# A two-layer attention network on one core: bias table in array quarters, short statistics as GpSimd powers, a reordered feed-forward

## The chip, the cores and the metric

The kernel runs on one core of a Trainium2 chip. The metric is the device time of one execution in microseconds (us). A core has five engines that run their own instruction queues in order: TensorE (PE, matrix products), VectorE (DVE), ScalarE (ACT, functions by table), GpSimd (POOL) and SyncE (SP, which here issues most DMAs). Matrix products go to PSUM; everything else works in SBUF.

## The reference, cut to what matters

The input is eight images of 384 channels by 32 x 32 pixels, so N = 1024 tokens each, in float32.

```python
# layer 0: group norm (32 groups), attention with 8 heads of 48 and a relative bias
qkv = tokens(_gn(x)) @ qkv_w + qkv_b
attn = softmax(q * 48**-0.5 @ k.T + bias)      # bias[h, q, k] = gelu(rel @ mlp_w1 + b1) @ mlp_w2 + b2
x = x + from_tokens((attn @ v) @ proj_w + proj_b)
# layer 1: layer norm, attention with 6 heads of 64, q and k normalised per head (mean 0, std 1)
t = tokens(x)
t = t + attention(_ln_t(t))
# feed-forward on the layer norm of t: two products with sign weights, each followed by a scaling
h = gelu(clip(y1 * 128 / (max|y1| + 1e-5)))     # y1 = u @ sign(W1 - mean).T + b1, 384 -> 1536
t = t + clip(y2 * 128 / (max|y2| + 1e-5))       # y2 = h @ sign(W2 - mean).T + b2, 1536 -> 384
```

The scalings take the largest value over groups of images of size 8 // 5 = 1, five groups; images 5 to 7 get zeros from the feed-forward, which the kernel leaves out for them. `bias` depends only on the difference of two pixel positions, so it is a table of 63 x 63 = 3969 values a head, of which each (query, key) block reads a window.

## The kernel before, in words

All tiles have 128 partitions; a product tile of PSUM holds 128 x 1024 float32 and there are four of them in each layer. Both layers run under `manual_schedule`, so every engine runs its instructions in the order in which the program's text issues them. A helper `later` holds pieces of work: `later.after(n, f)` runs `f` at the n-th following `later.step()`, and a step is made after every product unit, projection or feed-forward step.

Tiles come from pools with a fixed number of buffers. In layer 0 the pool `a_e` has nine buffers (`etile`): the exponentials `e`, the windows `wide`, the broadcast reciprocals `rb` and the residuals `res` share them. In layer 1 the pool `b_work` has 17 (`wtile`). A tile takes a buffer at its first write in program order and gives it back after its last use in program order; the next tile to take that buffer waits for that last use.

**Layer 0, start.** `bias_table` (line 205) goes over the 3969 positions in eight pieces of 512. Each piece makes two products of the 2-row `rel` with `w1` (line 213), two gelus (L223), two products with `w2` into 8 rows (L230), an addition (L234) and a DMA to the table in DRAM. The steps of the first group norm are called between the pieces. Then `grow_part(h, c)` reads windows of the table: four DMAs into `wide` (L246) and one reversed copy into `grow`, on ScalarE for even `c` (L252) and VectorE for odd `c` (L254). There are 32 such parts; eight are read during the first projections and the others between the first image's score units, just before they are needed.

**Layer 0, each image.** There are 32 units: four pairs of heads by eight key tiles. `scores` makes the products of a unit (L361), VectorE adds the bias into an `e` tile (L369) and ScalarE takes the exponential (L373); `weigh` multiplies with `v` two units later (L384, `LAG = 2`). After a pair's last unit `weigh` copies the sums out (L393), sends the denominators through DRAM (`sd`, `sums`, L399 and L401), takes the reciprocal two steps later (L404), sends it through DRAM again (`rd`, L406) into a broadcast tile `rb` (L409), and two steps after that GpSimd multiplies (L410). The group norm of the next image (`group_norm`) takes its square root on ScalarE (L284). Then come the next image's projections (L316 for queries and keys, L339 for values) and, in the fourth unit of the next image, the output projection (L421).

**Layer 1.** `center` prepares the weights. Each image has 24 units (three pairs by eight), with scores L1028, exponentials L1035, running totals on VectorE (L1042, L1045) and weighing L1056; `divide` sums the totals by a product (L1068) and divides as in layer 0 (L1086 to L1095). `project_qk` (L894) also squares its result (L908) for `head_sums` (L917); `normalise_qk` turns these into scales through DRAM: sqrt L938, reciprocal L939, `rq` and `kc` loads, and multiplies on GpSimd (L968). `token_sums` (L864) and `token_stats` (L881 to L887) make the layer norm's statistics; `scale_v` multiplies the values by them (L990).

For the first five images the feed-forward follows the attention, with the next image's projections set between its parts: `project_out` (L1104), `layer_norm` (L1148, L1149, and `halves`, which splits a tile in a high part, L1122, and a low part, L1124, for two fast products), `feed_forward_1` (L1185, evicted by L1170, largest value L1173, all-reduce on GpSimd L1159), then `quantised_gelu` for each of twelve chunks (VectorE scales L1198, GpSimd clips on both sides L1199, ScalarE gelu L1200, `halves`) and `feed_forward_2` (L1212).

Of the kernel before, what the change touches and what calls it, by code (L numbers as in the profile page):

```python
# [93 lines left out]
def _layer0(tc, ins, x1, flag):  # L94
# [6 lines left out]
    with ExitStack() as ctx:  # L101
# [18 lines left out]
        gn_eps = const.tile([GROUPS, 1], F32, tag="gn_eps", name="gn_eps")  # L120
        nc.vector.memset(gn_eps, 1e-5)


# [3 lines left out]
        rel = v[0:2].rearrange("p m h d -> p (m h d)")[:, 0:NREL]  # L127
        nc.sync.dma_start(rel, ins["rel"])
# [7 lines left out]
        w1 = const.tile([2, HID], F32, tag="w1", name="w1")  # L136
        b1 = const.tile([HC, 2], F32, tag="b1", name="b1")
        w2 = const.tile([HC, 2, H0], F32, tag="w2", name="w2")
        b2 = const.tile([H0, 1], F32, tag="b2", name="b2")
        nc.scalar.dma_start(w1, ins["L0_conv_mlp_w1"])  # L140
        with nc.allow_non_contiguous_dma(reason="a bias, once"):
            nc.scalar.dma_start(b1, ins["L0_conv_mlp_b1"].rearrange("(k p) -> p k", p=HC))
        nc.scalar.dma_start(w2, ins["L0_conv_mlp_w2"].rearrange("(k p) h -> p k h", p=HC))
        nc.scalar.dma_start(b2, ins["L0_conv_mlp_b2"].unsqueeze(1))
# [60 lines left out]
        def bias_table(between):  # L205

            starts = list(range(0, NREL, HALF))

            def hidden(at):
                n = min(HALF, NREL - at)  # L210
                ph = mm2(f"ph{at}")
                for k in range(2):
                    nc.tensor.matmul(
                        ph[0:HC, k, :n], w1[:, ts(k, HC)], rel[:, at : at + n], start=True, stop=True
                    )
                return ph

            ph = hidden(starts[0])
            for i, at in enumerate(starts):
                n = min(HALF, NREL - at)  # L220
                hid = etile(f"hid{at}", (HC, 2, HALF))
                for k in range(2):
                    nc.scalar.activation(  # L223
                        hid[:, k, :n], ph[0:HC, k, :n], AF.Gelu, bias=b1[:, k : k + 1]
                    )
                if i + 1 < len(starts):
                    ph = hidden(starts[i + 1])
                pb = mm2(f"pb{at}")
                for k in range(2):
                    nc.tensor.matmul(  # L230
                        pb[0:H0, 0, :n], w2[:, k, :], hid[:, k, :n], start=(k == 0), stop=(k == 1)
                    )
                part = etile(f"part{at}", (H0, HALF))
                nc.vector.tensor_scalar_add(backwards(part[:, n - 1 : n], n), pb[0:H0, 0, :n], b2)  # L234
                nc.sync.dma_start(table[:, NREL - at - n : NREL - at], part[:, :n])
                if i < len(between):
                    between[i]()
# [18 lines left out]
        def group_norm(b, xn):  # L256
# [25 lines left out]
            def scatter():  # L282
                nc.vector.bn_aggr(mv, gs)
                nc.scalar.activation(mv[:, 1:2], mv[:, 1:2], AF.Sqrt, bias=gn_eps)  # L284
                nc.vector.reciprocal(mv[:, 1:2], mv[:, 1:2])
                nc.vector.tensor_scalar(
                    mv[:, 0:1], mv[:, 0:1], mv[:, 1:2], -1.0, ALU.mult, ALU.mult
                )
                nc.vector.tensor_copy(of, mv.unsqueeze(1).to_broadcast([GROUPS, C // GROUPS, 2]))
                with nc.allow_non_contiguous_dma(reason="statistics"):  # L290
                    nc.sync.dma_start(
                        back.rearrange("(g r) s -> g (r s)", g=GROUPS),
                        of.rearrange("g r s -> g (r s)"),
                    )
                    nc.sync.dma_start(sc, back.rearrange("(k p) s -> p k s", p=P))
# [81 lines left out]
        def weigh(b, u, es):  # L377
# [24 lines left out]

            def invert():
                nc.vector.reciprocal(inv, mine)  # L404
                with nc.allow_non_contiguous_dma(reason="sums"):
                    nc.sync.dma_start(rd.rearrange("j (p c) -> (j p) c", c=2 * N // P), inv)  # L406
                rb = etile(f"rb{b}_{pair}")
                for j in range(2):
                    nc.sync.dma_start(rb[ts(j, S0)], rd[j].partition_broadcast(S0))  # L409
                later.after(2, lambda: nc.gpsimd.tensor_mul(o, o, rb))  # L410

            later.after(2, invert)
# [18 lines left out]
        with tc.manual_schedule():  # L431
            stages = group_norm(0, first)
            load_weights_qk()
            between = [stages[0], stages[1], stages[2], load_weights_v_out, stages[3], None, stages[4]]
            bias_table([w or (lambda: None) for w in between])
            nc.gpsimd.memset(v, 1.0)
            parts = [(h, c) for h in range(H0) for c in range(4)]
            for i in range(4):
                later.after(i + 1, lambda: (grow_part(*parts.pop(0)), grow_part(*parts.pop(0))))
            qk = project_qk(0, first)  # L440
            project_v(0, first)
            for b in range(B):
                held = []
                for i, u in enumerate(units):
                    if b == 0 and parts and i > 1:
                        for _ in range(2 if i < 6 else 1):
                            grow_part(*parts.pop(0))
# [319 lines left out]
def _layer1(tc, ins, x1, out):  # L767
    nc = tc.nc
    with ExitStack() as ctx:
# [46 lines left out]
        eps = const.tile([P, 1], F32, tag="eps", name="eps")  # L816
        nc.vector.memset(eps, 1e-5)
# [61 lines left out]
        def token_stats(name, c):  # L879

            nc.vector.tensor_scalar_mul(c, c, 1.0 / C)  # L881
            mean, var = c[:, 0], c[:, 1]
            sq = small.tile([P, MT], F32, tag="tq", name="tq" + name)
            nc.vector.tensor_mul(sq, mean, mean)
            nc.vector.tensor_sub(var, var, sq)
            nc.scalar.activation(var, var, AF.Sqrt, bias=eps)
            nc.vector.reciprocal(var, var)  # L887
# [37 lines left out]
        def normalise_qk(b, qk, d):  # L925
# [10 lines left out]

            def invert():
                nc.scalar.activation(c, c, AF.Sqrt, scale=1.0 / (D1 - 1))  # L938
                nc.vector.reciprocal(c, c)  # L939
                rqs = []  # L940
# [25 lines left out]
                def apply():  # L966
                    for pair in range(NP1):
                        nc.gpsimd.tensor_mul(qk[pair, 0], qk[pair, 0], rqs[pair])  # L968
                    nc.vector.tensor_scalar_mul(kc, kc, D1**-0.5)

                later.after(2, apply)

            later.after(2, invert)
            return kc

# [87 lines left out]
        def divide(b, oT, pair):  # L1063
# [20 lines left out]

            def invert():
                nc.vector.reciprocal(inv, inv)  # L1086
                with nc.allow_non_contiguous_dma(reason="sums"):
                    nc.sync.dma_start(spread(rd), inv)
                rb = wtile(f"rb{b}_{pair}")
                for j in range(2):  # L1090
                    nc.sync.dma_start(rb[ts(j, D1)], rd[j].partition_broadcast(D1))
                if pair < NP1 - 1:
                    later.after(2, lambda: nc.gpsimd.tensor_mul(oT[:, pair], oT[:, pair], rb))
                else:
                    later.after(1, lambda: nc.vector.tensor_mul(oT[:, pair], oT[:, pair], rb))  # L1095

            later.after(2, invert)
# [22 lines left out]
        def halves(name, t, high):  # L1120
# [3 lines left out]
            nc.vector.tensor_sub(low, t, high.bitcast(F32))  # L1124
            return high, low

        def layer_norm(b, xt, c):
# [3 lines left out]
            rows, parts = [], []  # L1131

            def spread():
                token_stats(f"f{b}", c)
                nc.vector.tensor_mul(c[:, 0], c[:, 0], c[:, 1])
                r = dram.tile([2, N], F32, tag="lr", name=f"lr{b}")
                with nc.allow_non_contiguous_dma(reason="statistics"):
                    nc.sync.dma_start(bass.AP(r.tensor, r.offset, [[MT, P], [N, 2], [1, MT]]), c)
                shift, scale = wtile(f"ls{b}"), wtile(f"lc{b}")
                nc.sync.dma_start(scale, r[1].partition_broadcast(P))  # L1140
                nc.sync.dma_start(shift, r[0].partition_broadcast(P))
                rows.extend((scale, shift))

            def apply():
                for k in range(KC):
                    eng = nc.gpsimd if k == 0 else nc.vector
                    t = wtile(f"un{b}_{k}")
                    eng.tensor_mul(t, xt[:, k], rows[0])  # L1148
                    eng.tensor_sub(t, t, rows[1])  # L1149
                    parts.append(halves(f"un{b}_{k}", t, high[:, k]))  # L1150

            return parts, spread, apply
# [44 lines left out]
        def quantised_gelu(name, y, r):  # L1197
            nc.vector.tensor_scalar(y, y, r, 1.0, ALU.mult, ALU.mult)  # L1198
            nc.gpsimd.tensor_scalar(y, y, QTOP, -QTOP, ALU.min, ALU.max)  # L1199
            nc.scalar.activation(y, y, AF.Gelu)  # L1200
            return halves(name, y, work.tile([P, N], F32R, tag="w", name="h" + name))

        def feed_forward_2(b, y1, r, made, xt):
# [194 lines left out]
```

## Time and profile before

| | |
|---|---|
| runs of before, us | 3776.57, 3784.86, 3781.83; median 3781.83 |
| profiled execution, us | 3782.44 |
| its span from the first to the last instruction, us | 3780.5 |
| mean granted TensorE clock | 0.953 |
| PE busy | 3464.5 us, 92% |
| DVE busy | 1652.6 us, 44% |
| ACT busy | 1471.3 us, 39% |
| POOL busy | 360.0 us, 10% |

The stages in the trace: the bias table's products run from 3.8 to 58.3 us, the first projections of layer 0 start at 58.7, its first scores at 115.6, and the second image's projections at 290.0. The later images of layer 0 follow each other every 201 us. Layer 1's weights load at 1742.5. Its feed-forward images take about 291 us each.

How to read the lines that follow. A line of the timeline gives start and duration in us, engine, source line, instruction, what it writes and reads, shapes and the number of instructions; in brackets, how long the engine had been idle before it and what ended that. A line of the waits gives the engine and tile that waited, what it waited for, the total in us, the number of times and the longest. A line of the windows gives start:end, length, then the busy time of PE, weight loads, DVE, ACT and POOL with their instruction counts, the granted clock, the DMA share and GB/s. Busy digits are tenths.

### The profile page before, as it was taken

How to read it: one execution, taken by the hardware profiler on the slowest of the kernel's cores; microseconds unless marked ns; L12 is line 12 of the kernel's file. 1: busy time of each engine (PE TensorE's matmuls, PEld its weight loads, DVE VectorE, ACT ScalarE, POOL GpSimd, SP SyncE). 2: the span in 40 equal slices, each digit the busy share in tenths (PEclk: the TensorE clock that was granted, in tenths of full speed). 3: DMA queues.
4: the chain of work that ended last, by engine and by line, in shares of the span. 5: the costliest groups of instructions: out<-in, count | busy, mean ns of one | idle time of the engine just before them, and what ended most of it. 6: DMA issues, size and time to landing. Idle time of an engine off the chain costs nothing. (4 is left out here: it accounts for less than half of the span.)

```text
span 3780.5 us, 31094 instructions
## 1 busy us (share of the span) xinstructions
PE 3464.5 (92%) x12170; PEld 1452.6 (38%) x12170; DVE 1652.6 (44%) x1667; ACT 1471.3 (39%) x1460; POOL 360.0 (10%) x259
## 2 busy tenths in 40 slices
PE   9889999999999999996987898799698698699998
PEld 2224343433333343432434434435334434434342
DVE  1452635353544445362434443543453453363434
ACT  2341524243433425250433443442453452352533
POOL 1010000000000001000100200200200200201010
PEclk9889999999999999998998999899899899899999
DMA  3321011010101010102300100100110010011011
GB/s 86 85 70 40 29 34 40 18 56 8 62 12 63 12 57 18 40 18 83 91 12 12 52 18 12 52 18 12 33 32 18 24 40 18 18 46 42 29 41 35
DMA packets 100428, 140.34 MB, mean 37 GB/s; under 512 B 61912, under 2 KB 65378, under 8 KB 100270
## 3 DMA queue, kind: packets, MB, share of 16 engines
q1 hardware_dynamic: 97484, 138.24, 12.6%
q8 instruction: 98, 1.61, 0.2%
q14 instruction: 58, 0.48, 0.0%
q10 hardware_dynamic: 2788, 0.02, 0.0%
HBM read 110.90 MB, written 27.32 MB: 37 GB/s over the span
## 5 line engine op out<-in xcount | busy, mean ns | idle before, releaser
L373 ACT ACTIVATE e<-e 128x1024 f32<-128x1024 f32 x512 | 538.5, 1056 | 655.1 <-DVE e L369 636.8
L369 DVE TENSOR_TENSOR e<-s,grow 128x1024 f32<-128x1024 f32 x512 | 600.4, 1216 | 269.0 <-PE s L361 226.9
L361 PE MATMUL s<-qk 48*128 48x512 f32 x2048 | 537.6, 623 | 34.0 <-DVE e L369 34.0
L1035 ACT ACTIVATE e<-s,kc 128x1024 f32<-128x1024 f32 x384 | 405.3, 1112 | 297.1 <-PE s L1028 276.6
L384 PE MATMUL o<-e,v 128*64 128x512 f32 x2048 | 502.8, 614 | 0.0
L1028 PE MATMUL s<-qk,qk 64*128 64x512 f32 x1536 | 398.8, 626 | 30.3 <-ACT e L1035 20.0
L1045 DVE TENSOR_TENSOR t<-t,e 128x1024 f32<-128x1024 f32 x288 | 352.3, 1268 | 167.2 <-ACT e L1035 167.2
L1056 PE MATMUL o<-e,v 128*64 128x512 f32 x1536 | 372.1, 608 | 0.0
L361 PEld LDWEIGHTS s<-qk 48*128 48x128 f32 x2048 | 187.2, 188 | 378.2 <-DVE e L369 201.9
L316 PE MATMUL pq<-xn,wqk 128*128 128x512 f32 x768 | 331.7, 593 | 0.0
L894 PE MATMUL pq<-bx,L_attn_qkv_wT 128*128 128x512 f32 x576 | 257.2, 600 | 8.0 <-DVE L_attn_qkv_wT L851 8.0
L384 PEld LDWEIGHTS o<-e,v 128*64 128x64 f32 x2048 | 126.8, 137 | 345.4 <-issue 204.9
L1028 PEld LDWEIGHTS s<-qk,qk 64*128 64x128 f32 x1536 | 142.1, 189 | 279.9 <-ACT e L1035 159.3
L410 POOL TENSOR_TENSOR oT<-oT,rb 128x1024 f32<-128x1024 f32 x32 | 75.8, 2368 | 1543.2 <-DMA rb<-rd 1463.9
L316 PEld LDWEIGHTS pq<-xn,wqk 128*128 128x128 f32 x768 | 145.3, 190 | 186.2 <-issue 186.2
L1212 PE MATMUL y2p<-hyh,w 128*128 128x512 f32 x360 | 138.7, 472 | 69.5 <-ACT hyh L1122 69.4
L1056 PEld LDWEIGHTS o<-e,v 128*64 128x64 f32 x1536 | 94.7, 137 | 256.9 <-issue 254.6
L1124 DVE TENSOR_TENSOR lyh<-y,hyh 128x1024 fp32r<-128x1024 f32 x60 | 73.7, 1228 | 266.4 <-ACT hyh L1122 266.4
L421 PE MATMUL pp<-oT,wp 128*128 128x512 f32 x384 | 169.0, 600 | 13.4 <-POOLq L1351 13.4
L894 PEld LDWEIGHTS pq<-bx,L_attn_qkv_wT 128*128 128x128 f32 x576 | 108.8, 192 | 149.9 <-issue 138.9
L1185 PE MATMUL y1p<-un,w 128*128 128x512 f32 x360 | 122.4, 423 | 37.1 <-ACT un L1122 37.1
L1200 ACT ACTIVATE y<-y 128x1024 f32<-128x1024 f32 x60 | 63.4, 1057 | 224.4 <-POOL y L1199 224.4
(142 smaller groups left out, 2910.4 us busy)
## 6 DMA issues: line engine op xcount, KB each, us to landing
rb<-rd SPq DMA_DIRECT2D x112, 256.0 KB
wide<-table SPq DMA_DIRECT2D x128, 114.2 KB
xn<-in_x_dram SPq DMA_DIRECT2D x24, 512.0 KB
res<-in_x_dram SPq DMA_DIRECT2D x24, 512.0 KB
x<-res SPq DMA_DIRECT2D x24, 512.0 KB
bx<-x SPq DMA_DIRECT2D x8, 1536.0 KB
rq<-hi SPq DMA_DIRECT2D x48, 256.0 KB
out_dram<-bx SPq DMA_DIRECT2D x24, 512.0 KB
```

The source lines that it names most:

```text
L316: nc.tensor.matmul(pq[:, h], wqk[:, k, s * H0 + 2 * pair : s * H0 + 2 * pair + 2, :].rearrange("p h d -> p (h d)"), xn[:, k, ts(h, HALF)], ...
L361: nc.tensor.matmul(s[j][:, h], qk[pair][rows, 1, ts(mt, P)], qk[pair][rows, 0, ts(h, HALF)], start=True, stop=True,)
L369: nc.vector.tensor_add(e, flat2(s[j]), grow[:, 2 * pair + j, w0 : w0 + IH, :].rearrange("p w c -> p (w c)"),)
L373: nc.scalar.activation(e, e, AF.Exp)
L384: nc.tensor.matmul(po[ts(j, S0), h], v[:, mt, 2 * pair + j, :], es[j][:, ts(h, HALF)], start=(mt == 0), stop=(mt == MT - 1),)
L421: nc.tensor.matmul(pp[:, h], wp[:, k, ts(m, P)], oT[:, k, ts(h, HALF)], start=(k == 0), stop=(k == NP0 - 1),)
L894: nc.tensor.matmul(pq[:, h], wqkv[:, k, s * C + pair * P : s * C + (pair + 1) * P], xt[:, k, ts(h, HALF)], start=(k == 0), stop=(k == KC - 1),
L1028: nc.tensor.matmul(s[j][:, h], qk[pair, 1][rows, ts(mt, P)], qk[pair, 0][rows, ts(h, HALF)], start=True, stop=True,)
L1035: nc.scalar.activation(e, flat2(s[j]), AF.Exp, scale=kc[:, pair, j, mt : mt + 1])
L1045: nc.vector.tensor_add(total[pair, j], total[pair, j], e)
L1056: nc.tensor.matmul(po[ts(j, D1), h], v[:, mt, at : at + D1], es[j][:, ts(h, HALF)], start=(mt == 0), stop=(mt == MT - 1),)
L1212: nc.tensor.matmul(py[m][:, h], w2[:, k, ts(m, P)], parts[i][:, ts(h, HALF)], start=(k == 0 and i == 0), stop=(k == FC - 1 and i == 1),)
```

## The change

1. **Bias table.** `rel` and `w1` are loaded four times, at partitions 0, 32, 64 and 96, each copy of `rel` holding a quarter of the positions. The hidden products of four quarters use four row groups of the array; the output products write to four groups of 32 columns. The table is made in two rounds (`hidden`, `table_part`) with gelus of 96 x 1024. All 32 `grow_part`s are issued during the first projections, three a step for eight steps and two a step for four. `v`, whose memory held `rel`, is filled with ones at the start.
2. **Short statistics.** Square roots (ScalarE) with reciprocals (VectorE) become powers of -0.5, and the reciprocals of the divisions powers of -1, as two-input instructions on GpSimd: 128x16 in `weigh` and `divide`, 128x8 in `token_stats`, 128x96 in `normalise_qk`, 32x1 in `group_norm`. In `weigh` and in layer 1's first two divisions the power, the DMAs behind it, the allocation of `rb` and the multiply are issued at once instead of by `later`.
3. **Feed-forward image.** `layer_norm` issues its statistics at once and makes its chunks in `begin` and `end`, between the next image's projections. `Supply` takes `quantised_gelu` apart: in step k of `feed_forward_2` come the low half of chunk k+1, the gelu and high half of k+2 and the clips of k+3. VectorE clips above with the scaling; the lower clip is on VectorE for the first three chunks, else on GpSimd. The last two chunks' products are grouped by output tile. The last pair of query and key projections moves behind `feed_forward_1`, the value projections ahead of `project_out`, and the last head sums behind the first products of `feed_forward_2`; the power of `normalise_qk` is issued in its third step and the multiplies in steps seven to nine.
4. **Images without feed-forward** issue the normalisation at once, and their value projections behind it. The start of layer 1 does the same.

The diff's core:

```diff
-        w1 = const.tile([2, HID], F32, tag="w1", name="w1")
+        QT, QN = 32, 2 * HALF
+        rel = etile("rel")
+        w1 = const.tile([P, HID], F32, tag="w1", name="w1")
...
+        for g in range(P // QT):
+            at = g * QN
+            n = min(QN, NREL - at)
+            nc.sync.dma_start(rel[g * QT : g * QT + 2, 0:n], ins["rel"][:, at : at + n])
+            nc.scalar.dma_start(w1[g * QT : g * QT + 2], ins["L0_conv_mlp_w1"])
...
+                        nc.tensor.matmul(
+                            ph[0:HC, i], w1[g * QT : g * QT + 2, ts(k, HC)],
+                            rel[g * QT : g * QT + 2, ts(r, HALF)], start=True, stop=True,
+                        )
...
+                    nc.tensor.matmul(
+                        pb[ts(g, QT), 0], w2[:, k, :], hids[k, g // 2][:, g % 2],
+                        start=(k == 0), stop=(k == 1),
+                    )
...
+            stages[0]()
+            hids.append(hidden(1))
+            for r in range(2):
+                table_part(r, hids[r])
+                stages[1 + r]()
+            load_weights_v_out()
+            for stage in stages[3:]:
+                stage()
...
+            for i in range(12):
+                later.after(i + 1, lambda i=i: grow_parts(3 if i < 8 else 2))
...
-                    if b == 0 and parts and i > 1:
-                        for _ in range(2 if i < 6 else 1):
-                            grow_part(*parts.pop(0))
...
-            def invert():
-                nc.vector.reciprocal(inv, mine)
...
-                later.after(2, lambda: nc.gpsimd.tensor_mul(o, o, rb))
-
-            later.after(2, invert)
+                nc.gpsimd.tensor_tensor(inv, mine, over.to_broadcast([P, 2 * N // P]), ALU.pow)
+                nc.sync.dma_start(rd.rearrange("j (p c) -> (j p) c", c=2 * N // P), inv)
+            rb = etile(f"rb{b}_{pair}")
+            for j in range(2):
+                nc.sync.dma_start(rb[ts(j, S0)], rd[j].partition_broadcast(S0))
+            nc.gpsimd.tensor_mul(o, o, rb)
...
-                nc.scalar.activation(c, c, AF.Sqrt, scale=1.0 / (D1 - 1))
-                nc.vector.reciprocal(c, c)
+                nc.gpsimd.tensor_scalar(c, c, 1.0 / (D1 - 1), 0.0, ALU.mult, ALU.add)
+                nc.gpsimd.tensor_tensor(c, c, rsqrt.to_broadcast(list(c.shape)), ALU.pow)
...
+            def clip(self, k):
...
+                nc.vector.tensor_scalar(y, y, self.r, QTOP, ALU.mult, ALU.min)
+                if k < 3:
+                    nc.vector.tensor_scalar_max(y, y, -QTOP)
+                else:
+                    nc.gpsimd.tensor_scalar(y, y, -QTOP, 0.0, ALU.max, ALU.add)
...
             for k in range(FC):
...
+                supply.low(k + 1)
+                supply.gelu(k + 2)
+                supply.clip(k + 3)
+                if k < FC - 2:
+                    for m in range(KC):
+                        products(k, m)
+                if k == 0:
+                    between()
                 later.step()
...
+                    supply = Supply(b, *feed_forward_1(b, un))
+                    supply.clip(0)
+                    supply.clip(1)
+                    supply.gelu(0)
+                    project_qk(b + 1, 2, 0, ahead, nqk, sq)
+                    supply.low(0)
+                    supply.clip(2)
+                    supply.gelu(1)
+                    project_qk(b + 1, 2, 1, ahead, nqk, sq)
+                    ways = []
+
+                    def between():
+                        head_sums(b + 1, 2, sq, d)
+                        ways.extend(normalise_qk(b + 1, nqk, d))
+                        later.after(3, ways[1])
+                        for pair in range(NP1):
+                            later.after(7 + pair, lambda pair=pair: ways[2](pair))
+
+                    feed_forward_2(b, supply, between, xt)
```

## The prediction

> **What bounds the kernel now.** I read the page first, then what TensorE waits for, then windows by stage, then the timeline around each wait. Slices of busy time and of granted clock:
>
> ```profile
> PE   9889999999999999996987898799698698699998
> PEclk9889999999999999998998999899899899899999
> ```
>
> TensorE is 92% busy, so only its holes and the half-clock time behind them can be won: the third slice, and layer 1 in slices 18 to 35. Its waits (what waited, on what: total, times, longest):
>
> ```profile
> PE y2p L1212 <- ACT hyh L1122: 69.4, 29, 6.1
> PE hs L917 <- ACT qsq L908: 66.2, 7, 13.7
> PE y1p L1185 <- ACT un L1122: 37.1, 15, 2.7
> PE s L361 <- DVE e L369: 34.0, 11, 13.5
> ```
>
> Three of the four lie in the feed-forward, five times each; the fourth is layer 0's first image. What a hole costs beyond itself, from the timeline (start, length):
>
> ```profile
> 169.82 3.78 PE L361 MATMUL s<-qk 48*128 48x512 f32 x6 [4.03 <-DVE e L369]
> 173.53 3.68 PE L384 MATMUL o<-e,v 128*64 128x512 f32 x8
> ...
> 179.19 1.94 PE L384 MATMUL o<-e,v 128*64 128x512 f32 x8
> ```
>
> After 4.03 us idle, six score products take 3.78 us instead of 1.49 and eight others 3.68 instead of 1.94: 4.0 us more. I add 4.0 us to a hole of 4 us or more, 2.5 to one of 3 to 4, about half its length to one over 10. [...]
>
> Two stages by windows (length, TensorE busy, ..., clock, DMA share, GB/s): a feed-forward image, and an image of layer 0.
>
> ```profile
> 2354.40:2646.40 292.00, 252.31 (x926) 126.73 (x924) 129.09 (x131) 120.78 (x120) 37.56 (x29) 0.92 0.09 27
> 489.00:690.00 201.00, 200.65 (x706) 74.93 (x704) 93.44 (x93) 77.92 (x75) 13.01 (x7) 1.00 0.12 35
> ```
>
> The first loses 40 us idle and 7% of clock (20 us); the periods average 291 us, and I count 58 us to be won in each. The second loses nothing: layer 0 after its first image can only get worse.
>
> **1. Bias table and early reads: -70 us.** Table matmuls (64 instructions, 28.6 + 27.0 us busy) fill TensorE from 3.8 to 59 us. Their number stays, but four row or column groups work at once. The scores, which use two, do eight in 1.92 us (0.24 each) against 0.43 for the whole-array projection: 1.8 times; for four I take 4 at best, 2 at worst, 14 to 28 us. With eight gelus of 1.06 us between, and loads and memsets to 6 us, the table stands at 23. Group norm's last statistics and gather are issued behind it; gather 3.5, then from its aggregate to the applied image 5.1 us as now (43.8 to 48.9): projection at 33 (28 to 40), not 58.7. Then the 128 window reads of 114.2 KB, which ran before at this rate (a window of 70 us from 50, 40 slices):
>
> ```profile
> DMA  0000005499999998000000000000000000000079
> GB/s 0 9 0 0 9 7 193 127 253 234 224 234 234 228 233 194 0 0 0 0 0 0 0 0 0 0 0 0 0 0 0 0 0 0 0 0 0 0 204 412
> ```
>
> 14.6 MB at 230 GB/s is 64 us, from 31 to 95. Copies stand ahead of evictions on VectorE and ScalarE, so adds begin at 98; TensorE is by then two units ahead, and with 4 us of clock the loop starts in effect at 99.5, not 115.6: 16. The first image's loop lasted 174.4 us, against 120.1 in the second (140.7 less 20.6 of output projection): 54. If reads run as slowly as 40 did from 117 (29.7 us), 39 us is left of the 70; if only TensorE binds, 80.
>
> **2. Layer 0's divisions: +226 us.** The reciprocal becomes a power on GpSimd, and the chain loses its delays. But rb is now taken from the nine-buffer pool at the division and released there in program order. Slots come back first in, first out (so they do in the buffers of the kernel before): with six e tiles held, rb's slot goes to the first e three units later. Before, taken one unit later and released two after that, it came back at six. The second division in image 1:
>
> ```profile
> 437.99 1.99 PE L361 MATMUL s<-qk 48*128 48x512 f32 x8
> ...
> 439.64 0.99 ACT L393 COPY oT<-o 128x1024 f32<-128x1024 f32 x1
> ...
> 443.92 0.25 DVE L404 RECIPROCAL inv<-sums 128x16 f32<-128x16 f32 x1 [1.49 <-DMA sums<-sd]
> ...
> 447.64 2.36 DVE L369 TENSOR_TENSOR e<-s,grow 128x1024 f32<-128x1024 f32 x2 [1.27 <-PE s L361]
> ...
> 450.88 2.38 POOL L410 TENSOR_TENSOR oT<-oT,rb 128x1024 f32<-128x1024 f32 x1 [21.17 <-DMA rb<-rd]
> ```
>
> Weighing ends at 438.0; the multiply ends at 453.3, or 14.8 + p after it in clean chains, p the power of 128x16. The add of three units on stood at 447.6, so it waits on the multiply; queued behind it on VectorE are all further adds. TensorE needs that add's PSUM at 449.6 (11.6) and gets it at 14.8 + p + 1.2: 4.4 + p lost, plus 4.0 of clock. Three pairs in each of eight images, 24 chains; the fourth pair's falls under the next projection.
>
> No row shows a power. Nearest: GpSimd's two-input multiply, 2368 ns for 1024 (2.3 ns an element a partition); its library routine PARTITION_ALL_REDUCE takes 380 ns for one. A power is a logarithm and an exponential, some 25 such operations: I take 60 ns, so 0.5 us for 128x8, 1.0 for 128x16, 5.8 for 128x96 (ends 0.2 and 36). The chains then cost 24 x (4.4 + 1.0 + 4.0). [...]
>
> **3. Feed-forward: -245 us.** Now each of twelve steps is one serial loop of clip 0.75, GpSimd clip 1.04, gelu 1.06, cast 1.04, low half 1.23, as the next clip is queued behind the low half:
>
> ```profile
> 2347.15 0.38 POOL L1159 PARTITION_ALL_REDUCE qt<-qm  x1 [47.44 <-DVE qm L1157]
> 2354.89 1.03 POOL L1199 TENSOR_SCALAR y<-y 128x1024 f32<-128x1024 f32 x1 [7.36 <-PE hs L917]
> ...
> 2374.51 1.04 POOL L1199 TENSOR_SCALAR y<-y 128x1024 f32<-128x1024 f32 x1 [5.48 <-DVE y L1198]
> 2379.79 1.04 POOL L1199 TENSOR_SCALAR y<-y 128x1024 f32<-128x1024 f32 x1 [4.24 <-issue]
> ```
>
> That is 5.28 us a step; TensorE needs 2.80 (12 x 0.233). Spread over two steps it becomes 2.64: TensorE binds. GpSimd's 7.4 us after its all-reduce hides, as the first three clips run on VectorE (0.75 us each more) and the fourth is due 11 us later; two projections cover the rest, and the head sums (13.4 us wait) move behind the first products. The normalised chunks (7.9 us of waits) start a projection earlier: covered by about 1 us with the 0.5 power in the chain. The last pair's multiply, 1.95 us late now, has 12.0 us of cover for a chain of 11.95 (the tail's, sum to product) + 0.75: 1.3 lost. The 128x96 power stands among GpSimd's clips: 2.3 us are slack, 3.5 + 2.5 of clock lost; three multiplies of 2.4 beside clips of 1.04 in 2.8 us steps, 2. So 9 of the 58 stay: 49 x 5.
>
> **4. The rest: -10 us.** Images without feed-forward wait 7 us and 3.4 of clock for keys; after, cover 22.4 (sums, four value projections) against a chain of 19.8 + 6.3: 5.7 lost, -9 for two. Layer 1's start: 9.2 + 5 becomes 3 to 4 late plus clock, -7. In its first image the division blocks GpSimd between all-reduces of the sign weights; VectorE and ScalarE wait behind: 14 us instead of 8.3, +8. Layer 0's sqrt table loads lie on an idle ScalarE: nothing, but 0.35 a image, -2. Removing vector work gains nothing elsewhere (44% busy).
>
> Sum: -70 + 226 - 245 - 10 = -99. The profiled execution took 3782.4 (span 3780.5), 0.6 over the median: **3684 us**.
>
> **Rivals.** *The power decides (slower).* At 170 ns an element, 128x96 takes 16 us: feed-forward keeps 27 of 58 (-155), chains 12.1 each (+290), images without feed-forward +22, layer 1's start +7, first image +10, with -72 left of term 1 and the rest: +102, 3884. Between the two cases the sum moves 1.8 us a ns, so it decides from about 115 ns (11 us for 128x96). [...]
> *No slot wait.* If rb's slot returns later than I count, term 2 is gone: 3458. For it: layer 0 shows no wait of this kind now; against: the order of slots follows from the program.
> *Cheap power.* At 20 ns: chains 214, feed-forward 54 x 5, -95 for the rest: 3631; part of the forecast's range.
> *Early reads do not help* (slow reads, copies blocking evictions): 31 us more, 3715.
>
> **Chances.** Forecast with its bounds 0.48, power above its point 0.36, about even 0.06, no slot wait 0.10. The range 3600 to 3890 leaves out the no-wait case and the longest powers, under 0.2; the forecast alone spans 3610 to 3750. Changes of 0.2% (7.6 us) are what a measurement can tell. Faster 0.58, same 0.05, slower 0.37.
>
> **What would show it.** First scores near 98 us and no copies after them; 24 waits of s on e of 4 to 6 us in layer 0, with adds released by GpSimd's multiply three units after a division; powers near 1.0 and 5.8 us; y2p, hs and y1p waits under 30 us together. Wrong if layer 0 stays without waits, or if GpSimd's powers exceed 10 us.

## The result, and the profile after

The changed kernel takes 3888.12 us (median of four runs, 3884.31 to 3894.01) where the kernel before, on the same chip, takes 3783.11: a ratio of 1.0282, 95% interval 1.0264 to 1.0301. It is slower by 105 us; the forecast was 3684, 99 us faster. The profiled execution took 3884.31 (span 3882.5).

The page of the changed kernel, slices of TensorE's busy time and granted clock:

```profile
PE   7999999999999999996788798698798798698988
PEclk9999998999999998997889899899899899899999
```

The hole in the third slice is gone; layer 1 (from slice 20) has as many holes as it had. What TensorE waits for in the changed kernel (total, times, longest; `y2p` is the second feed-forward product, `s` a unit of scores, `hs` the head sums):

```profile
PE y2p L1253 <- ACT hy L1136: 127.6, 30, 16.2
PE s L379 <- DVE e L387: 65.3, 25, 3.7
PE s L1050 <- POOL qk L992: 52.9, 3, 18.7
PE hs L941 <- ACT qsq L932: 42.9, 17, 7.6
```

The waits on `un` (37.1 before) have left the top, and those on `qsq` shrank, but the second product waits 127.6 us instead of 69.4, layer 0's scores 65.3 over 25 places instead of 34.0, and the scores on their normalised queries up to 18.7 us. GpSimd's groups by shape tell why (busy us, mean ns of one):

```profile
L1230 POOL TENSOR_SCALAR y<-y 128x1024 f32<-128x1024 f32 x45 | 171.5, 3816 | 65.9 <-DVE y L1226 62.7 <-DMA rq<-hi 2.8
L965 POOL TENSOR_TENSOR hc<-hc,rsqrt 128x96 f32<-128x96 f32 x8 | 125.3, 15667 | 0.7
L420 POOL TENSOR_TENSOR inv<-sums,over 128x16 f32<-128x16 f32 x32 | 93.0, 2905 | 1326.0 <-DMA sums<-sd 1326.0
L911 POOL TENSOR_TENSOR tcf<-tcf,rsqrt 128x8 f32<-128x8 f32 x5 | 8.3, 1664 | 0.4
L303 POOL TENSOR_TENSOR gmv<-gmv,rsqrt 32x1 f32<-32x1 f32 x8 | 4.5, 562 | 0.7
```

The powers of lines 303, 911, 420 and 965 take 562, 1664, 2905 and 15667 ns for 1, 8, 16 and 96 elements a partition: about 0.4 us and 155 to 160 ns an element, where the forecast took 60. (In two other places the shapes of 16 and 8 average 3158 and 2163 ns.) The clip of line 1230 is the other surprise: 3.82 us, where the kernel before had a clip of 1.04. GpSimd is busy 846.7 us instead of 360.0.

The same two stages as before, by windows (length, PE, weight loads, DVE, ACT, POOL, clock, DMA share, GB/s):

```profile
2354.40:2641.20 286.80, 246.52 (x925) 123.92 (x924) 136.78 (x120) 116.02 (x114) 97.91 (x43) 0.92 0.09 27
236.00:454.60 218.60, 211.13 (x707) 76.90 (x705) 92.81 (x87) 75.84 (x73) 25.71 (x15) 0.96 0.10 32
```

The feed-forward image is 5 us shorter than the window shown before (four periods average 287.8 against 291.3), and an image of layer 0, which lost nothing before, now takes 218.6 instead of 201. (A period is the time from one image's second product to the next one's.)

One division of layer 0, from the timeline of the changed kernel (start, length; weighing ends at 389.5):

```profile
391.12 0.99 ACT L411 COPY oT<-o 128x1024 f32<-128x1024 f32 x1
...
391.55 2.35 DVE L387 TENSOR_TENSOR e<-s,grow 128x1024 f32<-128x1024 f32 x2 [1.43 <-PE s L379]
...
395.34 2.36 DVE L387 TENSOR_TENSOR e<-s,grow 128x1024 f32<-128x1024 f32 x2 [1.43 <-PE s L379]
395.38 2.90 POOL L420 TENSOR_TENSOR inv<-sums,over 128x16 f32<-128x16 f32 x1 [17.23 <-DMA sums<-sd]
...
399.12 2.35 DVE L387 TENSOR_TENSOR e<-s,grow 128x1024 f32<-128x1024 f32 x2 [1.43 <-PE s L379]
...
404.51 2.34 POOL L425 TENSOR_TENSOR oT<-oT,rb 128x1024 f32<-128x1024 f32 x1 [6.22 <-DMA rb<-rd]
...
406.88 2.36 DVE L387 TENSOR_TENSOR e<-s,grow 128x1024 f32<-128x1024 f32 x2 [5.41 <-POOL oT L425]
...
408.16 2.67 PE L379 MATMUL s<-qk 48*128 48x512 f32 x6 [2.44 <-DVE e L387]
```

The multiply ends 17.4 us after the weighing (14.8 + 2.9 was the formula's 17.7), and an add does wait for it. But it is the fourth add after the division (391.55, 395.34, 399.12, then 406.88), not the third: the gap is 2.44 us.

In the feed-forward the 128x96 power stands among the clips (timeline of the changed kernel):

```profile
2460.67 3.63 POOL L1230 TENSOR_SCALAR y<-y 128x1024 f32<-128x1024 f32 x1 [0.63 <-DVE y L1226]
2464.38 0.59 POOL L964 TENSOR_SCALAR hc<-hc 128x96 f32<-128x96 f32 x1
2465.05 15.68 POOL L965 TENSOR_TENSOR hc<-hc,rsqrt 128x96 f32<-128x96 f32 x1
2480.73 7.22 POOL L1230 TENSOR_SCALAR y<-y 128x1024 f32<-128x1024 f32 x2
...
2486.57 1.22 PE L1253 MATMUL y2p<-hy,w 128*128 128x512 f32 x2 [16.22 <-ACT hy L1136]
```

The next clip waits for it, then gelu, cast and TensorE (16.22 us idle from 2470). Ahead of it and behind it a step takes 4.3 us, a clip and the 0.7 us until its input is there.

### The profile page after: what moved, and what is told of

Its sections match the earlier page's. It is cut to its first block, busy times and chain, and to the rows that moved or that the text cites. A ratio compares the mean times of both kernels' runs of the same rounds, so it can differ in the third digit from the quotient of the medians.

```text
span 3882.5 us, 31018 instructions
## 1 busy us (share of the span) xinstructions
PE 3467.2 (89%) x12170; PEld 1454.5 (37%) x12170; DVE 1684.4 (43%) x1522; ACT 1416.8 (36%) x1386; POOL 846.7 (22%) x432
## 3 DMA queue, kind: packets, MB, share of 16 engines
q1 hardware_dynamic: 97496, 138.24, 12.1%
## 4 chain that ended last, share of the span: by engine, by line
PE 32%; POOL 7%; DVE 4%; DMA 4%; issue 3%; ACT 2%; SPq 1%; POOLq 0%; DVEq 0%; ACTq 0%
PE s L1050 9%; PE o L1078 9%; PE y1p L1203 4%; PE pq L918 3%; PE pp L1118 3%; POOL hc L965 3%; POOL y L1230 2%; PE pv L1002 1%; PE y2p L1253 1%; DMA rb<-rd 1%; DVE y L1226 1%; DVE qk L926 1%; DVE un L1157 1%; DVE ly L1138 1%; DMA lc<-lr 1%
## 5 line engine op out<-in xcount | busy, mean ns | idle before, releaser
L379 PE MATMUL s<-qk 48*128 48x512 f32 x2048 | 571.9, 640 | 65.3 <-DVE e L387 65.3
L402 PE MATMUL o<-e,v 128*64 128x512 f32 x2048 | 534.6, 647 | 0.0
L1067 DVE TENSOR_TENSOR t<-t,e 128x1024 f32<-128x1024 f32 x288 | 380.4, 1366 | 160.6 <-ACT e L1057 160.3
L420 POOL TENSOR_TENSOR inv<-sums,over 128x16 f32<-128x16 f32 x32 | 93.0, 2905 | 1326.0 <-DMA sums<-sd 1326.0
L1078 PE MATMUL o<-e,v 128*64 128x512 f32 x1536 | 373.3, 608 | 2.3 <-POOL v L1012 2.3
L1253 PE MATMUL y2p<-hy,w 128*128 128x512 f32 x360 | 133.5, 456 | 127.6 <-ACT hy L1136 127.6
L1106 POOL TENSOR_TENSOR inv<-inv,over 128x16 f32<-128x16 f32 x24 | 75.8, 3158 | 545.9 <-DMA inv<-sd 521.8
L1230 POOL TENSOR_SCALAR y<-y 128x1024 f32<-128x1024 f32 x45 | 171.5, 3816 | 65.9 <-DVE y L1226 62.7
L434 PE MATMUL pp<-oT,wp 128*128 128x512 f32 x384 | 168.8, 600 | 17.9 <-POOLq L1428 17.9
L1138 DVE TENSOR_TENSOR ly<-y,hy 128x1024 fp32r<-128x1024 f32 x60 | 75.6, 1260 | 212.0 <-ACT hy L1136 212.0
```

The lines of the kernel that those rows point to most:

```text
L379: nc.tensor.matmul(s[j][:, h], qk[pair][rows, 1, ts(mt, P)], qk[pair][rows, 0, ts(h, HALF)], start=True, stop=True,)
L402: nc.tensor.matmul(po[ts(j, S0), h], v[:, mt, 2 * pair + j, :], es[j][:, ts(h, HALF)], start=(mt == 0), stop=(mt == MT - 1),)
L1067: nc.vector.tensor_add(total[pair, j], total[pair, j], e)
L1078: nc.tensor.matmul(po[ts(j, D1), h], v[:, mt, at : at + D1], es[j][:, ts(h, HALF)], start=(mt == 0), stop=(mt == MT - 1),)
L1230: nc.gpsimd.tensor_scalar(y, y, -QTOP, 0.0, ALU.max, ALU.add)
L1253: nc.tensor.matmul(py[m][:, h], w2[:, k, ts(m, P)], supply.parts[k][i][:, ts(h, HALF)], start=(k == 0 and i == 0), stop=(k == FC - 1 and i ...
```

## The experiments

The theory to be tested: two prices, that of the powers and that of the new clip, turned the gain into a loss, and the new order is good. The rivals: the order of queues or the place of `rb`'s buffer does it whatever the prices are. Medians are of four runs or more (one run for the price list); "less" is against 3888 unless another kernel is named. The kernel before, measured again beside the experiments, took 3782.2 to 3783.0.

**1. The clip's form.**

```diff
-                    nc.gpsimd.tensor_scalar(y, y, -QTOP, 0.0, ALU.max, ALU.add)
+                    nc.gpsimd.tensor_scalar(y, y, QTOP, -QTOP, ALU.min, ALU.max)
```

> The changed kernel with one edit: GpSimd's lower clip of chunks 3 to 11 (max, then add 0.0; 3.8 us in the changed kernel) is written as the kernel before had it (min, then max; 1.04 us there). Theory 'prices' (the powers and this slow form of the clip ate the gain): the steps of the second product fall from 4.3 us to what TensorE needs, 2.8, but for the 16 us power among them; some 20 us in each of five feed-forward images, 3790 (3770 to 3820), and the clip takes 1.04 us. Rival 'order' (the new order itself keeps TensorE waiting, on VectorE's and ScalarE's queues or on the power, whatever the clip takes): at most 20 us in all, 3870 or more. Rival 'neighbours' (the clip is slow since VectorE now works beside it): the clip stays above 2 us and the time at 3888.

Measured: 3822.73, 65 less, just above the theory's range; feed-forward periods 273.2 instead of 287.8. The waits of the second product on its high parts, in this kernel:

```profile
PE y2p L1253 <- ACT hy L1136: 79.2, 10, 13.5
```

The clip now takes 1.05 us at the median, so its neighbours are not what made it slow, and it is a cause; but 15 us an image were won, not 20: each still waits 13.5 us for the power.

**2. Layer 0's power.**

```diff
-                nc.gpsimd.tensor_tensor(inv, mine, over.to_broadcast([P, 2 * N // P]), ALU.pow)
+                nc.gpsimd.tensor_tensor(inv, mine, milli.to_broadcast([P, 2 * N // P]), ALU.mult)
```

> The changed kernel, with layer 0's 128x16 power replaced by a multiplication by a constant on the same engine, in the same place of its queue; the reciprocal of layer 0's sums is left out by this. Theory 'prices': the multiply by rb then ends 15.0 us after the weighing instead of 17.4, the add that takes rb's buffer (four units after the division) is due at 15.4, and the 24 gaps of 2.3 to 2.8 us and the 3.4 us of half clock behind each go: 24 x 5 = 120 less, 3768 (3750 to 3790). Rival 'slot' (the buffer's place makes the add late whatever the power takes, as the DMAs are the most of the chain): gaps over 1 us remain in all 24 places and no more than 40 is won, 3848 or more.

Measured: 3763.54, 125 less. The multiplication takes 0.23 us, and the waits on the adds have all but gone:

```profile
PE s L381 <- DVE e L389: 6.6, 10, 2.1
```

Images of layer 0 follow each other every 203.7 us on average, instead of 220.0 (starts of projections, images 2 to 8). "Prices" is right here; the early buffer with a short power costs little: layer 1 starts 24 us later than with the bias table alone (1722.3 against 1698.0, experiment 7).

**3. The 128x96 power.**

```diff
-                nc.gpsimd.tensor_tensor(c, c, rsqrt.to_broadcast(list(c.shape)), ALU.pow)
+                nc.gpsimd.tensor_tensor(c, c, milli.to_broadcast(list(c.shape)), ALU.mult)
```

> The changed kernel, with the 128x96 power of the query and key norms replaced by a multiplication by a constant on the same engine, in the same place; the inverse root of these sums is left out by this. Theory 'prices': in the feed-forward the 16.2 us wait and the clock behind it go, less what the slow clips keep: 18 x 5 = 90; in the two images without feed-forward and at layer 1's start the waits of 18.7, 18.5 and 15.6 us go with their clock, 20 each: 60; together 150 less, 3738 (3710 to 3770). Rival 'order': behind the power the next clip, low half or projection is late anyway; no more than 50 less, 3838 or more.

Measured: 3777.73, 110 less: more than the rival allows, 40 short of the theory. Feed-forward periods are 273.1 (15 won each, not 18): the slow clips hold part of what the power leaves, as 51.7 us of y2p waits remain in 28 pieces of up to 4.4 us. The images without feed-forward take 168.8 instead of 184.7 (16 won, not 20); scores still wait up to 3.3 us there.

**4. All prices low.** The edits of 1, 2 and 3, and layer 1's 128x16 and 128x8 powers replaced in the same way.

> The changed kernel with the clip of the first experiment and all powers but group norm's 32x1 replaced by multiplications by constants (the reciprocals and inverse roots are left out by this): the new order and the new bias table with cheap short statistics. Theory 'prices': layer 0 120 less, feed-forward images 288 to about 247 us each (200 less), the images without feed-forward and layer 1's start 60 to 70 less: 3490 to 3510, under the kernel before by 270. The prediction's own sum for cheap powers was 3631. Rival 'order': over 3650, as the order of layer 0's slots and of the feed-forward keeps its own waits.

Measured: 3535.36, 353 less, and a ratio of 0.9344 (0.9328 to 0.936) to the kernel before; 25 above the theory's range, far below the rival's. A feed-forward image takes 253.4 us on average, not 247. One of them by windows, in this kernel:

```profile
2200.00:2453.40 253.40, 241.28 (x932) 122.43 (x928) 140.91 (x121) 115.98 (x114) 47.91 (x43) 0.97 0.11 31
```

So the order with cheap statistics is worth 38 us an image (32 in experiment 8, where no root is left out), and the prices ate all but 3.5 of it. In the feed-forward the two costs partly hide each other: clip alone 14.6, power alone 14.7, both (with the small powers) 34.4 an image.

**5. The place of rb's buffer, the power kept.**

```diff
+            def invert():
                 nc.gpsimd.tensor_tensor(inv, mine, over.to_broadcast([P, 2 * N // P]), ALU.pow)
...
+                later.after(2, lambda: nc.gpsimd.tensor_mul(o, o, rb))
+            later.after(2, invert)
```

> The changed kernel with one edit: layer 0's division keeps its 2.9 us power, but it, rb's allocation and the multiply are issued through later.after(2) and later.after(2), as in the kernel before. Theory 'price and place together': the wait needs both the long power and rb's early buffer; with rb taken two units later and released two after that, its buffer comes back about six units on, some 8 us after the multiply's end at about 18 us, so the 24 gaps go: 24 x 5 to 6, 3755 (3740 to 3780). Rival 'price alone' (the multiply delays TensorE through something else than the buffer, for example the DMAs or GpSimd's queue): 3870 or more. The second experiment already excludes that the place alone does it (its 24 gaps went with the power).

The edit delays the power, its DMAs, the buffer and the multiply together.

Measured: 3729.67, 158 less; layer 0's images take 199.5 us on average instead of 220.0, 6.8 less for each of three divisions, and none of the kernel's twelve largest waits is of scores on adds. With experiment 2 this shows a conjunction: a short power with the early buffer, or the long power with a late buffer, costs little or nothing; only both together make the 24 waits. The theory's 120 to 145 was too low; 199.5 is also 4.2 below experiment 2, of which the 6.6 us of wait left there are only a part; the rest is open.

**6. The price list of the clip.** One form a chunk:

```diff
+                elif k == 3:
+                    nc.gpsimd.tensor_scalar(y, y, QTOP, -QTOP, ALU.min, ALU.max)
+                elif k == 4:
+                    nc.gpsimd.tensor_scalar(y, y, -QTOP, QTOP, ALU.max, ALU.min)
...
```

> The changed kernel, with another form of GpSimd's lower clip for each of the chunks 3 to 11 (op pairs min-max, max-min, max-mult, add-max, mult-max, max-max, a single max, mult-add, and max-add as it was); chunk 10 goes without its lower clip. A price list by line: theory 'pair' (the pair of operations sets the price): the pairs seen at 1.04 to 1.2 us in other places (min-max in the kernel before, mult-add for the group norm's images) keep that, max-add stays at 3.6 us, and the list shows which others are slow. Rival 'place' (the clip is slow for what runs beside it in the new order): all forms lie at 3.6 us or above.

The groups of this kernel by shape; the lines are, in the order of their numbers, min-max, max-min, max-mult, add-max, mult-max, max-max, max alone, mult-add, max-add:

```profile
L1230 POOL TENSOR_SCALAR y<-y 128x1024 f32<-128x1024 f32 x5 | 5.2, 1042 | 55.4 <-DVE y L1226 55.4
...
L1232 POOL TENSOR_SCALAR y<-y 128x1024 f32<-128x1024 f32 x5 | 18.4, 3681 | 11.2 <-PE y2p L1269 11.2
L1236 POOL TENSOR_SCALAR y<-y 128x1024 f32<-128x1024 f32 x5 | 18.2, 3648 | 0.0
L1234 POOL TENSOR_SCALAR y<-y 128x1024 f32<-128x1024 f32 x5 | 18.2, 3640 | 0.4
L1238 POOL TENSOR_SCALAR y<-y 128x1024 f32<-128x1024 f32 x5 | 18.2, 3633 | 0.4
L1240 POOL TENSOR_SCALAR y<-y 128x1024 f32<-128x1024 f32 x5 | 18.1, 3627 | 3.5 <-DVE y L1226 3.5
L1242 POOL TENSOR_SCALAR y<-y 128x1024 f32<-128x1024 f32 x5 | 13.9, 2776 | 3.5 <-DMA rq<-hi 2.1 <-DVE y L1226 1.4
L1244 POOL TENSOR_SCALAR y<-y 128x1024 f32<-128x1024 f32 x5 | 7.5, 1508 | 0.0
L1246 POOL TENSOR_SCALAR y<-y 128x1024 f32<-128x1024 f32 x5 | 22.5, 4493 | 0.4
```

Only min-max (1.04) and mult-add (1.51 here, 1.19 for group norm's images) are short; the same two clips in the other order, max-min, take 3.68, and a single max 2.78. The pair of operations sets the price. Each form stands at one chunk only; but max-add never took under 3.6 us at any of the nine chunks of the changed kernel, and min-max had a median of 1.05 over the same nine in experiment 1, so the place does not decide. (The whole kernel took 3869.64.)

**7. The bias table alone.** The kernel before, with the first part of the change only (the diff's core as shown above, without its powers).

> The kernel before with the bias table's part alone: rel and w1 at four row groups, two rounds, the 32 window reads during the first projections; divisions, square roots and layer 1 are those of before. The prediction's first term stands alone here: 70 less, 3713 (reads as slow as 40 us of the first image's were: 39 less, 3744; TensorE alone binding: 80 less, 3703). In the changed kernel the second image's projections started 54 us earlier with three slow divisions in that image.

Measured: 3713.48, 69 less than the kernel before's 3782.17. Projections of the second image start at 223.0, 67 us earlier. Term 1 stands.

**8. What the runs point to.** The clip of 1, layer 0's division as before, and the edits below; in the images without feed-forward the last division and two of the value projections also move ahead of the first multiply of `normalise_qk`.

```diff
-                nc.gpsimd.tensor_scalar(c, c, 1.0 / (D1 - 1), 0.0, ALU.mult, ALU.add)
-                nc.gpsimd.tensor_tensor(c, c, rsqrt.to_broadcast(list(c.shape)), ALU.pow)
+                nc.scalar.activation(c, c, AF.Sqrt, scale=1.0 / (D1 - 1))
+                nc.vector.reciprocal(c, c)
...
-                    invert()
+                    later.after(1, invert)
```

> The changed kernel without its costly parts: the clip of the first experiment; layer 0's division as in the kernel before (reciprocal on VectorE, by later); the 128x96 inverse root by ScalarE's square root and VectorE's reciprocal, issued one projection later than now in the images without feed-forward and at layer 1's start, in step three as now in the feed-forward. The 128x8 and layer 1's 128x16 powers stay on GpSimd. Nothing is left out. Theory 'prices': near the kernel with cheap statistics (3535): layer 0 some 10 less as its multiplies have no wait at all, layer 1 20 to 40 more for the remaining powers and for two table loads of 1.3 us in each feed-forward: 3560 (3530 to 3600). Rival 'order': square roots on ScalarE within the gelus stop the second product's steps: over 3650.

Measured: 3555.19, ratio 0.9395 (0.9379 to 0.941) to the kernel before. The sum fits the expectation, its parts do not: layer 0 ends 40 us earlier than in experiment 4 (1689.5 against 1729.3; 10 were expected), and what follows takes 55 longer (20 to 40 expected). Square roots among the gelus cost the second product's steps nothing that can be seen: its waits on the high parts are 14.2 us in all, 14.0 in experiment 4. The largest of the waits in total:

```profile
PE hs L946 <- ACT qsq L937: 43.4, 17, 7.6
```

**9. One chunk moved from GpSimd to VectorE.** Experiment 8 with:

```diff
-                normal(2, nc.gpsimd)
+                normal(2, nc.vector)
```

> The kernel of the run before it in this list (slow clip, layer 0's power and the 128x96 power replaced), with one more edit: the third normalised chunk's multiply and subtraction go from GpSimd to VectorE. Theory 'neighbours': in the changed kernel VectorE's subtraction takes 3.25 us beside GpSimd's 3.21 to 3.36 us pair, against 1.23 alone, and the evictions of the projections behind it make the head sums wait 7 us in each feed-forward image; four VectorE instructions of 1.23 us take less than the two slowed ones and the wait shrinks to under 3 us: 5 x (5 + 2 of clock) = 35 less than that kernel. Rival 'work': VectorE gets two more instructions ahead of the same evictions, and the wait stays: within 8 us of it.

Measured: 3551.5, 4 less than experiment 8, whose runs overlap with these; hs still waits up to 7.3 us. The slowing is real: beside GpSimd's pair VectorE's subtraction took 3.25 us (changed kernel),

```profile
2386.74 3.36 POOL L1156 TENSOR_TENSOR un<-bx,lc 128x1024 f32<-128x1024 f32 x1 [5.92 <-DMA lc<-lr]
2387.94 3.25 DVE L1157 TENSOR_TENSOR un<-un,ls 128x1024 f32<-128x1024 f32 x1
2390.18 3.21 POOL L1157 TENSOR_TENSOR un<-un,ls 128x1024 f32<-128x1024 f32 x1
```

and without it 1.23 (this kernel):

```profile
2443.56 1.23 DVE L1162 TENSOR_TENSOR un<-un,ls 128x1024 f32<-128x1024 f32 x1
```

But two more instructions take the time back (VectorE's four take 4.8 us, the two beside GpSimd took 4.4), and the rival "work" holds: what the head sums wait for is a square made behind the chunks, wherever these are made.

**10. The second head sums moved.** Experiment 8 with:

```diff
                 y1.append(y)
+                if m == 2:
+                    between()
...
-                    head_sums(b + 1, 1, sq, d)
-                    supply = Supply(b, *feed_forward_1(b, un))
+                    supply = Supply(
+                        b, *feed_forward_1(b, un, lambda: head_sums(b + 1, 1, sq, d))
+                    )
```

> The best kernel so far (slow clip, layer 0's power and the 128x96 power replaced; 3555) with one more edit: the second pair's head sums move behind the third tile of the first feed-forward product. In that kernel they are the longest wait of a feed-forward image (7.6 us, for a square that ScalarE makes after the normalised chunks). Theory: the first product's tiles need only the chunks, so TensorE goes on 6 us earlier and keeps its clock: 5 x (6 + 3.4) = 47 less, 3508 (3500 to 3530). Rival: the chunks themselves are late, and the wait goes over to the first product: no more than 15 less.

Measured: 3520.36, 35 less than experiment 8, ratio 0.9305 (0.9289 to 0.932) to the kernel before. The hs wait has fallen from 43.4 us to 2.6, and a third of it has come back on the first product:

```profile
PE y1p L1208 <- ACT un L1141: 9.1, 5, 2.1
...
PE y1p L1208 <- DVE lun L1143: 6.7, 5, 1.4
```

This is the fastest of the kernels, some 7% under the one before. Its longest single waits are none of the feed-forward's: 18.2 us of scores on exponentials in layer 1's first image and 17.0 of the first projections on the group norm.

## Why the prediction was wrong, point by point

The parts in the changed kernel, from the starts of stages: layer 0 ends (layer 1's first projection) at 1848.0, with the bias table alone at 1698.0, before at 1766.4.

| term | forecast, us | measured, us | from |
|---|---|---|---|
| 1 bias table, early reads | -70 | -68 | 1698.0 - 1766.4 |
| 2 divisions of layer 0 | +226 | +150 | 1848.0 - 1698.0 |
| 3 feed-forward | -245 | -17 | five times 287.8 - 291.3 |
| 4 the rest | -10 | +38 | what is left of 3882.5 - 3780.5 = 102 |

**Term 1 held** as forecast: experiment 7 measured 69 for it alone. In the changed kernel the first projection starts at 37.8 (forecast 33, 28 to 40), the first scores at 96.1, the first adds at 100 (forecast 98). The table's 64 products, now in four groups, keep TensorE busy for 16.0 us (4.7 to 20.7) instead of 54.3: 3.4 times less, where the forecast took 2 to 4.

**The step that failed is the price of the power**, taken at 60 ns an element: the multiply's 2.3 ns times 25 plain operations, a count that was the author's guess and that no run shows. The rows measure 155 to 160 and a base of about 0.4 us; the text named "GpSimd's powers exceed 10 us" as what would make it wrong, and 128x96 takes 15.7. The rival "the power decides" (170 ns, 3884) had the mechanism, and its condition (from about 115 ns) was met. It lies within 4 us of the result, but by luck: it gave layer 0 +290 and the feed-forward -155, against +150 and -17, so two errors of some 140 us cancelled. (Its 12.1 us a chain are also more than the forecast's own formula gives at 170 ns: 4.4 + 2.7 + 4.0 = 11.1, 267 in all.)

**Term 2's second step failed too**, the place of `rb`'s buffer: with the measured power its formula gives 24 x (4.4 + 2.9 + 4.0) = 271, and 150 was measured, 6.3 a chain (and 220.0 against 201.1 with the bias table alone, 6.3 for each of an image's three). The buffer comes back at the fourth add, not the third, so TensorE needs it one unit of 3.8 us later, at 15.4: 17.4 + 1.2 - 15.4 makes 3.2 late, 2.44 of it seen as a gap, and the 4.0 of clock is about right (6.3 - 2.4 = 3.9). With the right place the forecast's own 1.0 us power would have been 14.8 + 1.0 + 1.2 - 15.4 = 1.6 late, 38 us in all if the clock stays up. No run has this case: at 0.23 us the chains cost 24 us in experiment 2 and 31 in experiment 4, and in the kernel before one hole of only 0.96 us was followed by a granted clock of 0.50 for 6.8 us (143.3 to 150.1). The wrong place raised the sum, the wrong price lowered it.

**Term 3** had an unpriced step: the clip was taken over at 1.04 us, the row of the min-max clip before, though the code changes its pair to max-add. That is 3.8 us in nine of twelve steps. The order itself did what was said, in part: with short statistics and the old clip an image takes 253.4 us, 38 won of 49 forecast. Of the missing 11, the wait of hs on qsq is the largest piece: only the last head sums moved behind the first products, the second pair's still stood ahead of the first feed-forward product and waited 7.6 (6.6 to 7.1 in experiment 4). Moving them won 7.0 of the period (259.6 to 252.6, experiments 8 and 10).

**Term 4** went with the same price: 18.7 and 18.5 us of wait in the images without feed-forward and 15.6 at layer 1's start, each with a 15.7 us power in its chain (the forecast had 5.8; and its 19.8 + 6.3 against 22.4 is 3.7 late, so its 5.7 holds 2.0 that it does not name). The rival's 22 + 7 + 10 for this term and the first image agrees with the 38 measured. A part is no price, though: in layer 1's first image scores waited 16.6 us on exponentials (8.3 before, 14 forecast), still 14.2 in experiment 4, and 17.5 and 18.2 in experiments 8 and 10.

**Other rivals.** "No slot wait" is refuted by the timeline line at 406.88. "Early reads do not help" is refuted by experiment 7. "Cheap power" gave 3631 for 20 ns an element; multiplications in the powers' place, with the old clip, took 3535 (experiment 4): the chains cost 31 there (1729.3 - 1698.0 at layer 1's first projection), not 214, and the feed-forward won 190, not 270.

## What to carry to other kernels

A row prices an instruction only for its operation and pair of operations (on one shape 1.04 us for min-max and 3.68 for max-min): where a change touches these, bound the cost anew, and do so before all else for an engine that other steps queue behind. An early buffer and a long chain can each cost little and much only together (24 us with the short power, none with the late buffer, 150 with neither), so count units until the buffer's next user before pricing the chain. When a large reorder comes out slower, exchange its new instructions for cheap ones in the same place: here that one run separated a good order (253 us an image) from two bad prices.

## What the runs showed that was not expected

- GpSimd's two-input power: about 0.4 us plus 155 to 160 ns for each element of a partition, in four shapes.
- GpSimd's two-operation instruction on 128x1024: 1.04 us for min-max, 1.19 to 1.51 for mult-add, 3.6 to 3.7 for five other pairs, 2.78 for a single max. Max-add took 3.63 with VectorE idle beside it (at 2193.83 in the changed kernel), 3.82 on average there and 4.49 in experiment 6.
- GpSimd's small instructions (128x8 and 128x16) took 0.20 to 0.27 us alone and 1.06 to 1.17 us beside VectorE's two-input instructions (2392.2 to 2399.2 in the changed kernel); a pair of 128x1024 two-input instructions took 3.25 us instead of 1.23 on VectorE and 3.21 to 3.36 on GpSimd, where layer 0's multiply by rb takes 2.34. In experiment 9's lines of the changed kernel VectorE's subtraction ends 1.1 us after GpSimd's first instruction (2390.10), about its own 1.23, and GpSimd's second ends 2.2 after that subtraction (2391.19). What the two engines wait for in each other was not shown.
- A hole of 2.44 us in layer 0's scores was followed by slow products too (six in 2.67 us instead of 1.49): with 6.3 us a chain, about 3.9 lie behind the hole. The granted clock was 0.50 for 6.7 us behind this one (409.4 to 416.1), which is 3.4 us of them. The forecast had counted 4.0 only for holes of 4 us or more, and none under 3. Its other counts were the author's estimates. In the kernel before, 0.50 lasted 3.4 us behind one hole of 3.25 us (2126.5 to 2129.9) and 6.6 us behind another (2416.8 to 2423.4), so 1.7 and 3.3 were lost where 2.5 was counted; behind the 13.4 us hole that ends at 2367.8 it lasted 4.4 us, so 2.2 were lost and not half the hole's length.
- The first image's length differed by some 6 us between kernels with the same layer 0: the second image's projections start at 236.0 in the changed kernel and at 240.1 to 242.2 in experiments 1, 3 and 6, and at 225.8 in experiment 2 and 231.3 in 4. Why is open; the 150 us of term 2, from one trace each, are good to about that.
